# Convolutions that skip time steps by a branch, a written order for TensorE, and a moved set of copies, in a state-space and expert kernel

## The chip, the cores and the metric

The kernel runs on one core of one Trainium2 chip. The core has a matrix engine (TensorE, PE in the profile), a vector engine (VectorE, DVE), a scalar engine (ScalarE, ACT), a general engine (GpSimd, POOL) and an engine that mostly issues transfers (SyncE, SP). They run side by side, each through its own queue in order, and meet at semaphores. Matrix products go to a small memory (PSUM) that the other engines empty. The metric is the device time of one execution in microseconds (us): the median of the runs.

## The reference

The input x has 128 rows of 32 heads with 512 time steps each, and every row has a length. Each head's signal is convolved with a kernel made of 64 decaying waves, the skip term D is added, steps from the row's length on are set to zero, and the 4,096 tokens (row, head) of 512 numbers go through a mixture of 16 experts, of which each token takes 4, and one shared expert. The result is added to x.

```python
K = 2.0 * einsum('hn,hnl->hl', Ct, exp(P)).real          # one kernel per head
y = irfft(rfft(u, 2L) * rfft(K, 2L))[..., :L] + u * D[:, None]
y = y * (arange(L)[None, :] < length[:, None])[:, None, :]
scores = sigmoid(t @ gate_w.T) + bias                    # t: y as 4096 tokens of 512
topk_w, topk_idx = top_k(scores, 4); topk_w = topk_w / sum(topk_w)
out  = sum over the 4 experts e of topk_w[e] * (silu(t @ Wg[e].T) * (t @ Wu[e].T)) @ Wd[e].T
out += silu(t @ Sg.T) * (t @ Su.T) @ Sd.T                # the shared expert
return x + out
```

Lengths are drawn from 78 to 453; the longest of the 128 that are drawn is 443.

## The kernel before

**Kernels of the convolution.** `waves` and `kernels` make the 32 convolution kernels in five chunks (`CHUNKS`): long chains of VectorE operations with some on GpSimd, two sines on ScalarE, small TensorE products (L404), a VectorE addition into `krow` (L412). The result goes to memory (`kd`), and `kernel_strip` reads it back as a strip in which each partition is shifted by one step (L430), four heads at a time. Two strips are kept.

**Convolutions.** The heads go in eight blocks (`tb`) of four (`q`). `load_xt` brings a block of x with time on the partitions (L152). `convolve` multiplies one head: four products (L553) into one PSUM tile `py`, of 512, 384, 256 and 128 columns. The columns are time steps in falling order, column 0 is the last step, so the steps behind a row's end come first. VectorE multiplies the tile by `within`, the zeros behind each row's end (L560). Four transposes by TensorE (L563) with the matrix `to_rank` put the rows in order of length, and ScalarE copies them into `yT` (L564). A finished block goes out to `y_rows` (L899).

**Gates.** Behind a block, `gates` multiplies it by the gate weights (L584, tile `parts`), ScalarE copies that into `by_head`, and `sums` adds it up per head (L601, tile `pg`). Behind every second block `route` picks four experts per token: one long chain of VectorE operations from L623 to L656 (tile `cw`). `weights_out` puts the weights `cw` back into the order of rows by a TensorE product (L664, tile `cw_ps`), which ScalarE copies and SyncE stores in `y_rows` (L669). `ranks` makes small tables from the lengths, among them `k_u` (L512): for each group of 16 rows, how many slices of 128 steps they reach.

**Copies of x.** GpSimd's queue copies x into the output (L903), 1 MB for each block of heads: those of blocks 0 to 3 behind `tb` 3 to 6, the other four behind `tb` 7 (`COPIES`). Everything that is added to the output later waits for them.

**Units and tiles.** Behind the convolutions the shared expert runs in eight units (`unit_step`: `up` L967, `down` L982, added to the output L991), while tables for the sorted tokens are made (`slots`, called `making` there). `up` takes the number of slices from a register that TensorE loads from `k_u` (L1014) and branches on it (`by_tiles`, L942 and L943). Then come the experts: tiles of 128 tokens that share an expert, one `turn_of` each, with a gather four tiles ahead (L932), transposes (L1060, L1110), products (L1092, L1118), and the addition to the output (L1128). 134 tiles are used; those above `NT_MIN` = 128 are run one by one under a condition (`rest`).

**What sets the order.** In the part of the convolutions a scheduler of the tile framework sets each engine's order: it may move an operation past others that don't depend on it, and it does so with TensorE's products. So a `weights_out` that stands right behind `route` in the code is run some heads later. From `unit_step(0)` on the order is written out (`manual_schedule`).

Of the kernel before, what the change touches and what calls it, by code (L numbers as in the profile page):

```python
# [38 lines left out]
P = 128  # L39
# [19 lines left out]
NT_MIN = B * H * TOPK // P  # L59
QC = P // KT  # L60
# [16 lines left out]
def ssm_moe_kernel(  # L77
# [384 lines left out]
    key_col = const.tile([P, 1], F32, tag="key_col", name="key_col")  # L462
    for key, raw, own in ((key_row, key_row, cpos), (key_col, len_col, ppos)):
        nc.vector.tensor_scalar(key, raw, 0.0, float(L), ALU.max, ALU.min)
        if key is key_col:
            num_len = const.tile([P, 2], F16, tag="num_len", name="num_len")
            behind(nc.vector.tensor_copy(num_len[:, 0:1], ppos))
            nc.vector.tensor_copy(num_len[:, 1:2], key)
        nc.vector.scalar_tensor_tensor(key, key, float(P), own, ALU.mult, ALU.subtract)
# [14 lines left out]

    def ranks():
# [7 lines left out]
        nc.vector.tensor_copy(by_rank, by_rank_ps)  # L493

# [15 lines left out]
        nc.tensor.matmul(k_u_ps, lhsT=reach_b, rhs=unit, start=True, stop=True)  # L510
        k_u = const.tile([1, NU], I32, tag="k_u", name="k_u")
# [13 lines left out]
        )  # L525
        row_ps = ps_m.tile([P, NU], F32, tag="m", name="row_ps")
# [14 lines left out]
        return by_rank, reach, k_u, unit_rows  # L541
# [4 lines left out]


    def convolve(tb, q, xt, yb):
        h = tb * HB + q
        py = ps_g.tile([P, L], F32, tag="g", name=f"py{h}")  # L550
        for jt in range(KT):

            nc.tensor.matmul(  # L553
                py[:, : L - jt * P],
                lhsT=xt[:, jt, q, :],
                rhs=strip[tb][:, q, jt * P :],
                start=(jt == 0),
                stop=(jt == KT - 1),
            )
        nc.vector.tensor_mul(yb[:, q, :L], py, within)  # L560
        pt = ps_u.tile([P, KT, P], F32, tag="u", name=f"pt{h}")
        for kt in range(KT):
            nc.tensor.transpose(pt[:, kt, :], yb[:, q, kt * P : (kt + 1) * P], to_rank)  # L563
        return nc.scalar.copy(  # L564
            yT[:, :, :, h, :].rearrange("p u k b -> p k u b"),
            pt.rearrange("p k (u b) -> p k u b", u=NU),
        )
# [307 lines left out]
    xb = load_xt(0)  # L875
    nc.sync.dma_start(out=w_sh, in_=w_all[E])

    COPIES = {3: (0,), 4: (1,), 5: (2,), 6: (3,), 7: (4, 5, 6, 7)}
# [3 lines left out]
    made_waves, strips = {}, [1]  # L882
    for tb in range(NB):
        if tb == 2:
            by_rank, reach, k_u, unit_rows = ranks()
        yb = yp.tile([P, HB, L], F32, tag="yb", name=f"yb{tb}")
        x_next = load_xt(tb + 1) if tb + 1 < NB else None
        for q in range(HB):
            turned = convolve(tb, q, xb, yb)
            h = tb * HB + q  # L890
            if h in waves_at:
                made_waves[waves_at[h]] = waves(*waves_at[h], 0)[0]
            if h in kernels_at:
                kernels(*kernels_at[h], *made_waves[kernels_at[h]])

            if strips[-1] in (tb, tb + 1) and strips[-1] < NB and strips[-1] * HB in kd_of:
                kernel_strip(strips[-1])
                strips.append(strips[-1] + 1)
        nc.scalar.dma_start(out=y_bh[:, tb * HB : (tb + 1) * HB, :L], in_=yb)  # L899

        for part in COPIES.get(tb, ()):
            own = slice(part * HB, (part + 1) * HB)
            x_out = nc.gpsimd.dma_start(out=out_bh[:, own, :], in_=x[:, own, :])  # L903
            dep(x_out, turned, "behind the block")
        gates(tb)
        if tb + 1 < NB:
            sums(tb)
            if tb % RB == RB - 1:
                route(tb // RB)
                weights_out(tb // RB)  # L910
        xb = x_next
# [47 lines left out]
    k_us, adds, loads = {}, [], []  # L959
# [49 lines left out]
    def unit_step(u):  # L1009
# [3 lines left out]
        if u < NU:  # L1013
            k_us[u] = nc.tensor.value_load(k_u[0:1, u : u + 1], min_val=1, max_val=KT)  # L1014
# [135 lines left out]
    with tc.manual_schedule(engines=None):  # L1150
# [37 lines left out]
        for step in range(1, NT_MIN + 2):  # L1188
            turn_of(step)
# [64 lines left out]
```

## Time and profile before

| | us |
|---|---|
| median of 3 runs (933.74 to 934.65) | 934.33 |
| profiled execution | 936.54 |
| its span | 934.8 |
| TensorE busy in the span | 887.1 |
| VectorE busy | 411.9 |
| GpSimd busy | 419.8 |
| start of the first convolution product L553 | 22.66 |
| start of the weights products L664 at blocks 1, 3 and 5 | 69.38, 100.35, 128.32 |
| start of the first product of the units L967 | 138.64 |
| end of the last addition to the output issued by GpSimd | 923.0 |

The span is the time from the first to the last instruction of the profiled execution; what lies around it is the difference to that execution's time, 1.7 us. In rows in order of time the first number is the start in us from the span's start, the second the duration, then come engine, line, operation and tiles; what stands in brackets is how long the engine had stood idle before and what ended that. "x8" says that eight records were merged. A float32 product of TensorE leaves two records. Lines are those of the kernel before.

### The profile page before, as it was taken

To read this page: it belongs to the slowest core of one execution; us is meant where nothing else is said; L and a number is where in the kernel's file an instruction comes from. 1 tells how busy PE (TensorE), PEld (TensorE's weight loads), DVE (VectorE), ACT (ScalarE), POOL (GpSimd) and SP (SyncE) were. 2 spreads that over 40 slices of the span, in tenths; PEclk is the share of its full clock that TensorE was granted. 3 is DMA by queue.
4 is the path that set the end of the run, shared out by engine and by line. 5 is a ranking of instruction groups with operands and counts; after the bars stand their busy time and mean duration, and the time that the engine had idled before them with its cause. 6 is when DMAs were issued, how large, how long until landed. Compare 5 with 4: busy or idle time off the path is not lost.

```text
span 934.8 us, 14577 instructions
## 1 busy us (share of the span) xinstructions
PE 887.1 (95%) x2976; PEld 444.1 (48%) x2976; DVE 411.9 (44%) x1452; ACT 190.2 (20%) x377; POOL 419.8 (45%) x366
## 2 busy tenths in 40 slices
PE   2999979999999999999999999999999999999993
PEld 1555644444444444444444444454445454444441
DVE  8984445677851233423343334333433333344331
ACT  1222221111222122212221122212211112122220
POOL 2200010223456455645564556545655445566553
PEclk9999999999999999999999999999999999999997
DMA  5478955386869666775678567756766656677664
GB/s 202 147 235 270 322 192 163 46 301 127 145 123 238 163 114 116 141 173 106 115 137 184 104 109 137 130 101 110 131 108 114 105 104 112 108 129 137 117 115 85
DMA packets 54689, 135.95 MB, mean 145 GB/s; under 512 B 12416, under 2 KB 12576, under 8 KB 50976
## 3 DMA queue, kind: packets, MB, share of 16 engines
q0 software_dynamic: 36256, 89.77, 52.3%
q1 hardware_dynamic: 14080, 36.15, 11.5%
q10 hardware_dynamic: 4224, 8.39, 2.3%
q8 instruction: 72, 1.18, 0.5%
q14 instruction: 57, 0.47, 0.2%
HBM read 288.08 MB, written 60.64 MB: 373 GB/s over the span
## 4 chain that ended last, share of the span: by engine, by line
PE 67%; issue 1%; SPq 0%; POOL 0%; DVE 0%; ACT 0%; POOLq 0%; DVEq 0%
PE g L1092 34%; PE o L1118 24%; PE m L1060 4%; PE u L1110 3%; PE o L982 1%; POOL out L1128 0%; SPq L1195 0%; POOL yg L932 0%; SPq L1143 0%; DVE zt L1104 0%; SPq L1178 0%; SPq L1179 0%; SPq L1180 0%; ACT sgt L1103 0%; DVE zT L1113 0%
## 5 line engine op out<-in xcount | busy, mean ns | idle before, releaser
L1092 PE MATMUL g<-store,yt 128*128 x742 | 343.1, 596 | 2.0 <-issue 1.7
L1128 POOL DMA_INDIRECT out<-ob,put x134 | 212.1, 1583 | 241.5 <-DVE junk L1067 202.4
L1118 PE MATMUL o<-store,zT 128*128 x536 | 252.0, 592 | 0.1
L1104 DVE SCALAR_TENSOR_TENSOR zt<-g,wt,sgt 128x256 f32<-128x256 f32 x135 | 65.3, 483 | 307.5 <-ACT sgt L1103 307.5
L1092 PEld LDWEIGHTS g<-store,yt 128*128 128x128 f32 x742 | 130.3, 190 | 119.0 <-issue 117.9
L1118 PEld LDWEIGHTS o<-store,zT 128*128 128x128 f32 x536 | 101.5, 190 | 129.0 <-issue 124.6
L932 POOL DMA_INDIRECT yg<-y_rows,get x140 | 138.1, 986 | 42.7 <-issue 29.9
L1127 DVE COPY ob<-o 128x512 f32<-128x512 f32 x134 | 92.7, 692 | 109.5 <-PE o L1118 102.2
L1066 ACT COPY yt<-m 128x512 f32<-128x512 f32 x136 | 79.7, 586 | 225.8 <-PE m L1060 224.0
L1103 ACT ACTIVATE sgt<-g 128x256 f32<-128x256 f32 x135 | 51.9, 384 | 269.7 <-PE g L1092 269.2
L991 POOL DMA_INDIRECT out<-ob,unit_rows x32 | 50.2, 1568 | 99.8 <-ACT ob L989 94.1
L1060 PEld LDWEIGHTS m<-ident,yg 128*128 128x128 f32 x373 | 48.6, 141 | 72.9 <-issue 72.7
L553 PE MATMUL py<-strip,xt 128*128 128x512 f32 (+3 forms) x256 | 76.8, 437 | 2.8 <-DMA strip<-kd 2.8
L1060 PE MATMUL m<-ident,yg 128*128 128x128 f32 x373 | 63.2, 273 | 0.7 <-issue 0.6
L982 PE MATMUL o<-store,z 128*128 128x512 f32 x128 | 57.7, 597 | 1.3 <-ACT yt L1066 1.3
L1113 DVE COPY zT<-u 128x256 f32<-128x256 f32 x134 | 56.3, 420 | 0.4 <-PE u L1110 0.4
L1110 PE MATMUL u<-ident,zt 128*128 128x128 f32 x268 | 51.2, 273 | 0.6 <-DVE zt L1104 0.6
L553 PEld LDWEIGHTS py<-strip,xt 128*128 128x128 f32 x256 | 42.1, 191 | 19.5 <-issue 11.1
L967 PE MATMUL g<-store 128*128 128x512 f32 x92 | 44.8, 623 | 3.1 <-issue 2.6
L967 PE MATMUL u<-store 128*128 128x512 f32 x92 | 42.2, 593 | 0.0
L842 DVE TENSOR_SCALAR cols<-tpos_h,stl,tok 128x143 f16<-128x143 f16 x128 | 41.4, 328 | 0.0
L903 POOL DMA_DIRECT2D out<-in_x x8 | 4.4, 558 | 78.0 <-ACT store L564 78.0
(279 smaller groups left out, 507.5 us busy)
## 6 DMA issues: line engine op xcount, KB each, us to landing
store<-in_w_all SPq DMA_DIRECT2D x143, 1536.0 KB
xt<-in_x_t SPq DMA_DIRECT2D x8, 1024.0 KB
y_rows<-yb ACTq DMA_DIRECT2D x8, 1024.0 KB
out<-in_x POOLq DMA_DIRECT2D x8, 1024.0 KB, 10.1
strip<-kd SPq DMA_DIRECT2D x7, 1024.0 KB
yg<-y_rows,get POOLq DMA_INDIRECT x140, 4.4
out<-ob,put POOLq DMA_INDIRECT x134, 4.9
strip<-kd SPq DMA_DIRECT2D x4, 256.0 KB
```

The costliest lines, as they stand in the source:

```text
L553: nc.tensor.matmul(py[:, : L - jt * P], lhsT=xt[:, jt, q, :], rhs=strip[tb][:, q, jt * P :], start=(jt == 0), stop=(jt == KT - 1),)
L932: nc.gpsimd.indirect_dma_start(out=at(yg, t), out_offset=None, in_=y_rows[:, :], in_offset=bass.IndirectOffsetOnAxis(ap=made["get"][:, t : ...
L967: nc.tensor.matmul(ps[it], lhsT=w_sh[:, c0 : c0 + P], rhs=yT[:, u, kt, :, :].rearrange("p h b -> p (h b)"), start=(kt == KT - n), stop=(kt ...
L982: nc.tensor.matmul(po, lhsT=at(zu, u)[:, it, q * P : (q + 1) * P], rhs=w_sh[:, c0 : c0 + L], start=(it == 0), stop=(it == IT - 1),)
L1060: nc.tensor.transpose(pt[:, q, :], at(yg, t)[:, q * P : (q + 1) * P], ident)
L1066: nc.scalar.copy(at(yt, t), pt)
L1092: mm = nc.tensor.matmul(pgu, lhsT=at(yt, t)[:, q, :], rhs=ring_flat[:, bass.ds(w0s[t] + q * 2 * I, 2 * I)], start=(q == KT - n), stop=(q = ...
L1104: nc.vector.scalar_tensor_tensor(at(zs, t), pgu[:, I:], at(wts, t), sg, ALU.mult, ALU.mult)
L1110: nc.tensor.transpose(at(p_z, t)[:, it, :], at(zs, t)[:, it * P : (it + 1) * P], ident)
L1118: mm = nc.tensor.matmul(po, lhsT=at(zts, t)[:, it, :], rhs=ring_flat[:, bass.ds(w0s[t] + WD + it * L, L)], start=(it == 0), stop=(it == IT ...
L1127: nc.vector.tensor_copy(ob, po)
L1128: add = nc.gpsimd.indirect_dma_start(out=out, out_offset=bass.IndirectOffsetOnAxis(ap=made["put"][:, t : t + 1], axis=0), in_=ob, in_offse ...
```

## The change

Seven things are different.

1. A register `skips` says how many slices of 64 steps (`TS`) lie behind the end of the longest row, 0 to 3. It is worked out from the lengths by a reduction and five small operations of VectorE. From head 2 on `convolve` branches on it (`by_number`, two comparisons) to one of four copies of its products, in which the first 64, 128 or 192 columns are left out. Two fixed PSUM tiles `pys` take the place of a new one for each head, so that columns that are left out hold old finite numbers, which `within` sets to zero.
2. TensorE's order in the part of the convolutions is the written one. Other engines keep the scheduler.
3. The transposes of a head (`turn_y`) stand behind the products of the next head.
4. What follows a head is in `behind_head`: `weights_out` at heads 12, 20 and 28; a step of `ranks` at heads 13 to 16; `gates` of the block before at its second head; `sums` and `route` of the block before at its third head, so `route` comes at heads 10, 18 and 26.
5. The register for `k_u` of unit 0 is loaded before the last head's transposes, no longer in `unit_step`.
6. All eight copies of x are issued behind the last head's transposes.
7. At step 124 GpSimd gets a `drain` ahead of its gather.

```diff
+LAST_DRAIN = NT_MIN - 4
+TS = 64
+SKIPS = 4
@@ the lengths
+        if key is key_row:
+            nc.vector.tensor_reduce(longest, key[0:1, :], AX.X, ALU.max)
...
+    nc.vector.tensor_scalar(longest, longest, -1.0, float(L), ALU.mult, ALU.add)
+    floor_div(longest, longest, TS)
+    nc.vector.tensor_scalar(skips, longest, float(SKIPS - 1), None, ALU.min)
@@ convolve
+    def by_number(m, lo, hi, some):
+        if lo == hi:
+            some(lo)
+            return
+        mid = (lo + hi) // 2
+        with tc.If(m > mid) as more:
+            by_number(m, mid + 1, hi, some)
+        with more.Else():
+            by_number(m, lo, mid, some)
+    pys = [ps_g.tile([P, L], F32, tag="g", name=f"py{i}") for i in range(2)]
...
-        py = ps_g.tile([P, L], F32, tag="g", name=f"py{h}")
-        for jt in range(KT):
-            nc.tensor.matmul(
-                py[:, : L - jt * P],
-                lhsT=xt[:, jt, q, :],
-                rhs=strip[tb][:, q, jt * P :],
...
+        py = pys[h % 2]
+        def products(n):
+            c0 = n * TS
+            for jt in range(KT):
+                nc.tensor.matmul(
+                    py[:, c0 : L - jt * P],
+                    lhsT=xt[:, jt, q, :],
+                    rhs=strip[tb][:, q, jt * P + c0 :],
...
+        if h < 2:
+            products(0)
+        else:
+            if not skip:
+                skip[0] = nc.tensor.value_load(skips[0:1, 0:1], min_val=0, max_val=SKIPS - 1)
+            by_number(skip[0], 0, SKIPS - 1, products)
         nc.vector.tensor_mul(yb[:, q, :L], py, within)
+    def turn_y(h, yb):
+        q = h % HB
         pt = ps_u.tile([P, KT, P], F32, tag="u", name=f"pt{h}")
@@ the loop over the heads
-    COPIES = {3: (0,), 4: (1,), 5: (2,), 6: (3,), 7: (4, 5, 6, 7)}
...
+    def behind_head(h):
+        tb, q = divmod(h, HB)
...
+        if 13 <= h <= 16:
+            next(rest_of_ranks, None)
+        if h >= RB * HB and h % (RB * HB) == HB and h // (RB * HB) > 0:
+            weights_out(h // (RB * HB) - 1)
+        if q == 1 and tb > 0:
+            gates(tb - 1)
+        last = h == H - 1
+        if q == 2 and tb > 0 and not (tb == NB - 1):
+            sums_and_route(tb - 1)
+        if h > 0:
+            turn_y(h - 1, ybs[(h - 1) // HB])
+        if last:
+            sums_and_route(tb - 1)
+            k_us[0] = nc.tensor.value_load(of_ranks["k_u"][0:1, 0:1], min_val=1, max_val=KT)
+            turned = turn_y(h, ybs[tb])
+            gates(tb)
+            return turned
+    def sums_and_route(tb):
+        sums(tb)
+        if tb % RB == RB - 1:
+            route(tb // RB)
+    with tc.manual_schedule(engines={mybir.EngineType.PE}):
+        for h in range(H):
...
+            convolve(tb, q, xbs[tb], ybs[tb])
+            if q == HB - 1:
+                nc.scalar.dma_start(out=y_bh[:, tb * HB : (tb + 1) * HB, :L], in_=ybs[tb])
+            turned = behind_head(h)
+    for part in range(NB):
+        own = slice(part * HB, (part + 1) * HB)
+        x_out = nc.gpsimd.dma_start(out=out_bh[:, own, :], in_=x[:, own, :])
+        dep(x_out, turned, "behind the convolutions")
@@ unit_step
-            k_us[u] = nc.tensor.value_load(k_u[0:1, u : u + 1], min_val=1, max_val=KT)
+            if u > 0:
+                k_us[u] = nc.tensor.value_load(k_u[0:1, u : u + 1], min_val=1, max_val=KT)
@@ the steps
+            if step == LAST_DRAIN:
+                nc.gpsimd.drain(fusable=False)
             turn_of(step)
```

More of the change, by code (lines that the diff above doesn't have):

```diff
@@ L462, in ssm_moe_kernel @@
     key_col = const.tile([P, 1], F32, tag="key_col", name="key_col")
+    longest = const.tile([1, 1], F32, tag="longest", name="longest")
     for key, raw, own in ((key_row, key_row, cpos), (key_col, len_col, ppos)):
         nc.vector.tensor_scalar(key, raw, 0.0, float(L), ALU.max, ALU.min)
+        if key is key_row:
+            nc.vector.tensor_reduce(longest, key[0:1, :], AX.X, ALU.max)
         if key is key_col:
@@ L483, in ssm_moe_kernel @@
     nc.vector.tensor_scalar(to_row, rank_ps[:, :B], ppos, None, ALU.is_equal)
+    of_ranks = {}
     def ranks():
@@ L493, in ranks @@
         nc.vector.tensor_copy(by_rank, by_rank_ps)
+        yield
         reach = const.tile([P, KT], BF16, tag="reach", name="reach")
@@ L510, in ranks @@
         nc.tensor.matmul(k_u_ps, lhsT=reach_b, rhs=unit, start=True, stop=True)
+        yield
         k_u = const.tile([1, NU], I32, tag="k_u", name="k_u")
@@ L525, in ranks @@
         )
+        yield
         row_ps = ps_m.tile([P, NU], F32, tag="m", name="row_ps")
@@ L540, in ranks @@
         )
-        return by_rank, reach, k_u, unit_rows
+        of_ranks.update(by_rank=by_rank, reach=reach, k_u=k_u, unit_rows=unit_rows)
+    skips = const.tile([1, 1], I32, tag="skips", name="skips")
+    nc.vector.tensor_scalar(longest, longest, -1.0, float(L), ALU.mult, ALU.add)
+    floor_div(longest, longest, TS)
+    nc.vector.tensor_scalar(skips, longest, float(SKIPS - 1), None, ALU.min)
     within = const.tile([P, L], F32, tag="within", name="within")
     behind(nc.vector.tensor_scalar(within, lpos, len_col, None, ALU.is_lt))
+    def by_number(m, lo, hi, some):
[8 more added lines that the diff above has]
+    pys = [ps_g.tile([P, L], F32, tag="g", name=f"py{i}") for i in range(2)]
+    skip = {}
     def convolve(tb, q, xt, yb):
         h = tb * HB + q
-        py = ps_g.tile([P, L], F32, tag="g", name=f"py{h}")
-        for jt in range(KT):
-            nc.tensor.matmul(
-                py[:, : L - jt * P],
-                lhsT=xt[:, jt, q, :],
-                rhs=strip[tb][:, q, jt * P :],
-                start=(jt == 0),
-                stop=(jt == KT - 1),
-            )
+        py = pys[h % 2]
[6 more added lines that the diff above has]
+                    rhs=strip[tb][:, q, jt * P + c0 :],
+                    start=(jt == 0),
+                    stop=(jt == KT - 1 or L - (jt + 1) * P <= c0),
+                )
+                if L - (jt + 1) * P <= c0:
+                    break
+        if h < 2:
[4 more added lines that the diff above has]
+            by_number(skip[0], 0, SKIPS - 1, products)
         nc.vector.tensor_mul(yb[:, q, :L], py, within)
+    def turn_y(h, yb):
+        q = h % HB
         pt = ps_u.tile([P, KT, P], F32, tag="u", name=f"pt{h}")
@@ L872, in slots @@
         yield
-    xb = load_xt(0)
-    nc.sync.dma_start(out=w_sh, in_=w_all[E])
-    COPIES = {3: (0,), 4: (1,), 5: (2,), 6: (3,), 7: (4, 5, 6, 7)}
     waves_at = {0: CHUNKS[1], 2: CHUNKS[2], 7: CHUNKS[3], 12: CHUNKS[4]}
     kernels_at = {0: CHUNKS[1], 5: CHUNKS[2], 10: CHUNKS[3], 16: CHUNKS[4]}
[L882 to L911, printed above, removed]
@@ new lines, in ssm_moe_kernel @@
+    made_waves, strips, k_us = {}, [1], {}
+    ybs, xbs, rest_of_ranks = {}, {0: load_xt(0)}, ranks()
+    nc.sync.dma_start(out=w_sh, in_=w_all[E])
+    def behind_head(h):
+        tb, q = divmod(h, HB)
+        if h in waves_at:
+            made_waves[waves_at[h]] = waves(*waves_at[h], 0)[0]
+        if h in kernels_at:
+            kernels(*kernels_at[h], *made_waves[kernels_at[h]])
+        if strips[-1] in (tb, tb + 1) and strips[-1] < NB and strips[-1] * HB in kd_of:
+            kernel_strip(strips[-1])
+            strips.append(strips[-1] + 1)
+        if 13 <= h <= 16:
[15 more added lines that the diff above has]
+            return turned
@@ new lines, in sums_and_route @@
+    def sums_and_route(tb):
[4 more added lines that the diff above has]
+        for h in range(H):
+            tb, q = divmod(h, HB)
+            if q == 0:
+                ybs[tb] = yp.tile([P, HB, L], F32, tag="yb", name=f"yb{tb}")
+                if tb + 1 < NB:
+                    xbs[tb + 1] = load_xt(tb + 1)
+            convolve(tb, q, xbs[tb], ybs[tb])
+            if q == HB - 1:
+                nc.scalar.dma_start(out=y_bh[:, tb * HB : (tb + 1) * HB, :L], in_=ybs[tb])
+            turned = behind_head(h)
@@ L912, in ssm_moe_kernel @@
+    for part in range(NB):
+        own = slice(part * HB, (part + 1) * HB)
+        x_out = nc.gpsimd.dma_start(out=out_bh[:, own, :], in_=x[:, own, :])
+        dep(x_out, turned, "behind the convolutions")
+    by_rank, reach, k_u, unit_rows = (of_ranks[k] for k in ("by_rank", "reach", "k_u", "unit_rows"))
     conv.close()
@@ L958, in ssm_moe_kernel @@
     p_o = homes(ps_o, "o", [P, L], 2)
-    k_us, adds, loads = {}, [], []
+    adds, loads = [], []
     def up(u, it, ps, w0):
```

## The prediction

> **What bounds the kernel now.** I read the stages first: busy time of each engine between the marks of the convolution part (columns: stretch, its length, then PE, weight loads, DVE, ACT and POOL busy with instruction counts, granted clock, DMA share, GB/s).
>
> ```profile
> 17.00:69.40 52.40, 48.36 (x252) 29.42 (x252) 49.05 (x200) 10.79 (x22) 10.30 (x24) 1.00 0.58 188
> 69.40:100.40 31.00, 30.06 (x162) 18.68 (x162) 16.46 (x60) 6.52 (x12) 1.34 (x2) 1.00 0.85 286
> 100.40:128.40 28.00, 26.36 (x131) 16.14 (x131) 14.71 (x50) 6.03 (x11) 1.06 (x2) 1.00 0.82 287
> 128.40:138.70 10.30, 7.08 (x46) 4.02 (x46) 1.38 (x2) 3.10 (x6) 2.04 (x4) 1.00 0.40 117
> 138.70:300.00 161.30, 156.64 (x490) 73.03 (x491) 94.16 (x388) 32.31 (x55) 57.54 (x40) 0.99 0.68 160
> ```
>
> Up to 69.4 us VectorE and TensorE are both nearly full (49.05 and 48.36 of 52.4), after it TensorE alone. From 138.7 on, TensorE is never short of work, and the change touches nothing there but a drain. So a shift of the first product of the units (L967, at 138.64) passes whole to the end, and the question is when that product starts.
>
> Second, the waits of TensorE, which are few: the scheduler has put other work into every gap.
>
> ```profile
> PE pt L563 <- DVE yb L560: 3.2, 4, 1.5
> PE py L553 <- DMA strip<-kd: 2.8, 3, 1.5
> ```
>
> Third, in order of time, TensorE and then VectorE between one `sums` and the `weights_out` that belongs to it:
>
> ```profile
> 113.25 0.96 PE L601 MATMUL pg<-gather_q,by_head 128*128 128x16 f32 x8
> ...
> 121.69 2.97 PE L553 MATMUL py<-strip,xt 128*128 128x384 f32 x10
> 124.50 0.60 PE L563 MATMUL pt<-to_rank,yb 128*128 128x128 f32 x4
> ...
> 128.32 0.49 PE L664 MATMUL cw_ps<-cw,to_row 128*128 128x128 f32 x2
> ```
>
> ```profile
> 114.25 0.29 DVE L623 TENSOR_SCALAR neg<-pg 128x128 f32<-128x128 f32 x1 [0.97 <-PE pg L601]
> ...
> 127.97 0.29 DVE L656 TENSOR_TENSOR cw<-s,free 128x128 f32<-128x128 f32 x1
> ```
>
> `route` is a chain of VectorE operations from L623 to L656. Its parts between the multiplications L560 last 1.92, 2.16, 2.19, 3.15 and 0.73 us, together 10.15. TensorE fills that time with four more heads before it comes to `cw_ps`.
>
> **The change, part by part.** *Shorter products.* The longest of the drawn rows has 443 of 512 steps, so (512 - 443)/64 floors to 1 and heads 2 to 31 leave out 64 columns in each of four products: 1,024 columns for 1,280. From 121.69 to 124.50 TensorE made five products of 1,664 columns: 1.69 ns a column. So a head's products fall from 2.16 to 1.72 us, 0.43 each, 12.9 over 30 heads if TensorE were the bound throughout.
>
> *Start to the first `cw_ps`.* It isn't: VectorE has the same work before that point, plus six one-element operations (about 0.1 each, 0.6), and from 17 us to 69.3 it idles only some 2.4 us in all. In the written order it also waits for TensorE more: the kernel products L404 of the third chunk now stand behind the transposes and products of head 10 (0.44 + 1.72 + 0.5 = 2.7, less 1.5 of VectorE work in between: 1.2), the sums behind those (0.6), and head 7 behind `parts` and sums (0.5). So `cw_ps` starts at 69.38 + 0.6 + 2.3 = 72.3: +2.9, with no gain from shorter products.
>
> *The written order.* `weights_out` is now two heads behind `route` (heads 10 and 12, 18 and 20, 26 and 28). In TensorE's order its product stands ahead of everything later and waits for L656. Between the end of the sums and it TensorE has two heads: 2 x (0.44 + 1.72) = 4.3 us. VectorE needs 10.15 plus three multiplications of 0.6, which stand within its chain: 12.0. TensorE stands still for 7.7 us, queued behind it the transposes of the head before and all products; who waits for those are VectorE's multiplications and ACT's copies. Only at the first of the three does other VectorE work come into it; its wait is about 10 us, already within the 72.3.
>
> From `cw_ps` at head 12 to that at head 20 TensorE does: itself 0.42, six transposes 2.64, six heads 10.32, two `parts` 2.0, two sums 1.62, kernel products 0.62, three small ones 0.3 = 17.9, then the 12.0: 29.9 for 30.97 before (69.38 to 100.35), -1.05. To head 28: 17.0 + 12.0 = 29.0 for 27.97, +1.03. From there to L967: 0.42 + four transposes 1.76 + three heads 5.16 + `parts` 1.0 + sums 0.81 = 9.15; then head 31's transposes to the end of `parts`, 2.37 as before (134.60 to 136.97), and two branches 0.35: 11.9 for 10.32, +1.55. The early load of `k_u` (up to 0.81, below) is in that: it runs under the sums. Both waits for strips fall away, for the copies have left these transfers (three of 1 MB for four in a block); in these sums they aren't counted. Sum so far: 2.9 - 1.05 + 1.03 + 1.55 = +4.4.
>
> *The clock.* What an idle TensorE costs afterwards, the seam of before shows, in stretches of 3.4 us and then in order of time:
>
> ```profile
> 135.60:139.00 3.40, 1.42 (x9) 0.46 (x10) 0.00 (x0) 0.84 (x2) 2.04 (x4) 1.00 0.97 317
> 139.00:142.40 3.40, 3.40 (x5) 1.35 (x4) 0.00 (x0) 0.00 (x0) 0.00 (x0) 0.50 0.95 369
> ```
>
> ```profile
> 138.64 5.39 PE L967 MATMUL g<-store 128*128 128x512 f32 x8 [1.67 <-issue]
> 148.20 3.60 PE L967 MATMUL g<-store 128*128 128x512 f32 x8
> ```
>
> A stretch with 1.42 of 3.4 us busy was followed by one at half clock, and eight records took 5.39 us for 3.60: 1.8 lost. The Trainium skill (TensorE: Matmul & The Clock Gate, "Why this matters for your kernels") asks only that no gap exceed about 3 us; here gaps of 0.68 and 1.67 were enough, so the row decides. By both, each new stop of 7.7 us or more costs about 1.8: 3 x 1.8 = +5.4. By the row alone the seam can also become free: it is now some 70% busy, and a stretch with 2.15 of 3.4 busy (132.2 to 135.6) was followed by full clock: -1.8. By the rule the seam has nothing to win, and the total would be 939.2 where the row gives 937.4. Bounds: 0, and 7.5 if each stop throttles for more than one stretch. Sum: +8.0.
>
> *Branches and loads*, from rows by line (shortest, median, longest ns):
>
> ```profile
> L943 PEldq COMPARE_BRANCH  x364: 65/179/346, 138.5 to 900.3; - x182
> L1198 PEldq COMPARE_BRANCH  x8: 70/73/4495, 892.5 to 925.2; - x8
> L1014 PEldq TENSOR_LOAD <-k_u x8: 302/408/814, 137.2 to 266.3; - x8
> ```
>
> The Trainium skill (Runtime: NRT & Kernel Launch, "Instruction fetch mechanics") warns that a taken branch to code that isn't loaded stops the engine for a fetch. The exit at L1198 shows it, 4.5 us; 30 heads of that would be +135. But L943 jumps over alternatives of this size 364 times at 0.18. I take L943: two branches a head lie under the 2 us of queued products, so nothing; if that cover is gone (behind each stop), 0.3 each, 1 us in all. The load of `skips` comes at head 2, where VectorE is the bound; uncovered it is 0.8.
>
> *Copies of x.* Eight on POOL's queue behind the last transposes, with no POOL work before the units' adds behind them. Before, four took from 137.7 to 151.1 (13.4 us). Eight take some 27 from about 145: 172. The first add, 174.5 before, comes near 182: hidden by 10 us. On SP, each store of weights waits for its `cw_ps`; the loads behind it belong to later blocks and have over 10 us.
>
> *The drain.*
>
> ```profile
> L1239 POOLq DRAIN  x1: 194/194/194, 0.4 to 0.4; - x1
> L1250 POOLq DRAIN  x3: 46/109/5547, 928.1 to 934.2; - x3
> ```
>
> The last 5.55 us of the kernel are a POOL drain, begun when every transfer had landed. The first drain, with none issued, took 0.19. If its time grows with the 314 software transfers since the last drain (140 gathers, 134 + 32 adds, 8 copies), 24 are left behind step 124: 0.6, saving 4.9; if fixed, nothing. I take 4.9, nearer to the first row. The new drain costs POOL about as much at step 124, hidden by four gathers ahead and five `ob` buffers (near 20 us).
>
> Sum: 8.0 - 4.9 = **+3.1 us**. The profiled execution took 936.54 (span 934.8), so 939.6; on the median of 934.33 that is **937.4**.
>
> **Rivals.** *The drain saves nothing*: 942.3. For it: it began with all data landed. *The clock stays up at the stops*, or the stops are shorter by as much: 937.4 - 5.4 = 932.0; for it only that the rule's window and the gaps' place are loose. *The weights don't hold TensorE* (the other side: faster): if the chain after the sums took under 4.3 us, products would bound from head 14 on: 18 x 0.43 = 7.7, strips 2.2, load and clock at the seam 3.0, drain 4.9, less the 0.6: 917. It breaks even with today's 28 us at a chain of 11 us, clock aside; against it stand 10.15 us of VectorE work without one wait. *Copies land late*: if eight take over 38 us, the first adds hold the `ob` buffers and TensorE: 945 or more; the 13.4 us of today's four speak against it.
>
> **How the numbers follow.** Likeliest case 0.45 (937.4, own range 934.5 to 941), fixed drain 0.32 (942.3), clock kept 0.11 (932), no stop 0.06 (917), late copies 0.06 (945). Faster by over 0.2% (under 932.5; 0.2% is about what the three runs can tell): 0.06 and half of 0.11. Within: the other half and the low end of the first, 0.18. The rest is slower. The range leaves out "no stop" and the far end of the late copies: 931.5 to 945.
>
> **What would show it.** TensorE waiting for L656 at its weights product three times, 7 to 10 us each, with half clock behind; no wait for strips; L553's columns at four fifths; L967 near 147; the last drain under 1 us. Wrong if those waits are under 4 us, or VectorE's part before the first of them ends well before 72 us.

## The result and the profile after

The changed kernel takes 948.65 us (median; 947.86 to 949.12). The kernel before takes 934.49 us (median of four). The ratio is 1.0146, with a 95% interval of 1.0126 to 1.0166: 14.2 us slower. The forecast had the sign and most of the mechanism, but its 937.4 us is too low, and the result lies 3.7 us above the upper end of its range.

First, the same stages as before, cut at the same events (the three weights products, now L711, and the first product of the units, now L1036). Columns: stretch, its length, then PE, weight loads, DVE, ACT and POOL busy with instruction counts, granted clock, DMA share, GB/s.

```profile
17.00:76.70 59.70, 45.03 (x238) 29.70 (x238) 48.90 (x206) 9.88 (x21) 10.29 (x24) 0.89 0.62 198
76.70:109.55 32.85, 25.58 (x149) 18.40 (x149) 15.73 (x59) 6.02 (x11) 0.00 (x0) 0.92 0.58 187
109.55:142.00 32.45, 25.17 (x131) 18.03 (x131) 14.75 (x50) 5.96 (x11) 0.00 (x0) 0.87 0.42 141
142.00:155.75 13.75, 12.74 (x71) 8.58 (x71) 2.08 (x3) 3.97 (x8) 1.14 (x2) 0.88 0.21 66
```

Read the lengths against 52.40, 31.00, 28.00 and 10.30 us before, and the clock against 1.00. TensorE's busy time fell by 3.3, 4.5 and 1.2 us in the first three stretches, although part of it was run at half clock. Each of them is nevertheless longer: what was added is idle time of TensorE. In the first stretch VectorE did the same work (48.90 us for 49.05) in 7.3 us more.

The waits of TensorE between 17 and 160 us (what waited, for whom; total us, times, longest) say where the idle time is.

```profile
PE cw_ps L711 <- DVE cw L703: 21.6, 3, 8.7
PE py L587 <- DMA strip<-kd: 3.9, 1, 3.9
PE pt L610 <- DVE yb L604: 1.7, 2, 0.8
```

The first line is the one that the forecast described; these three waits are called the stops below. The second is one that it had ruled out. In order of time, TensorE around head 8 and around the second stop (start, busy, instruction, idle time before it and what ended that):

```profile
46.47 0.61 PE L610 MATMUL pt<-to_rank,yb 128*128 128x128 f32 x4
50.99 3.86 PE L587 MATMUL py<-strip,xt 128*128 128x448 f32 x8 [3.91 <-DMA strip<-kd]
54.64 1.06 PE L610 MATMUL pt<-to_rank,yb 128*128 128x128 f32 x4
55.50 2.51 PE L587 MATMUL py<-strip,xt 128*128 128x448 f32 x8
...
109.55 0.79 PE L711 MATMUL cw_ps<-cw,to_row 128*128 128x128 f32 x2 [6.43 <-DVE cw L703]
110.14 1.06 PE L610 MATMUL pt<-to_rank,yb 128*128 128x128 f32 x4
110.99 3.73 PE L587 MATMUL py<-strip,xt 128*128 128x448 f32 x8
```

A head's eight records take 1.95 us at full clock. Behind both kinds of wait they take up to twice that. The chain on VectorE that the second stop waits for, from its first to its last operation, lasts 12.0 us:

```profile
97.50 0.29 DVE L670 TENSOR_SCALAR neg<-pg 128x128 f32<-128x128 f32 x1 [3.53 <-PE pg L648]
...
109.21 0.29 DVE L703 TENSOR_TENSOR cw<-s,free 128x128 f32<-128x128 f32 x1
```

Last, the drains of POOL (duration in ns: shortest, median, longest; first and last start): the one at step 124, and those at the end.

```profile
L1260 POOLq DRAIN  x1: 8771/8771/8771, 881.1 to 881.1; - x1
```

```profile
L1322 POOLq DRAIN  x3: 109/193/2020, 943.3 to 946.9; - x3
```

Put beside the forecast's sum, by the two profiled executions (us; the forecast's clock term of 1.8 a stop stands where the stop is):

| Part | Forecast | Measured |
|---|---|---|
| start to the first weights product | +2.9 | 69.38 to 76.70: +7.3 |
| to the second | -1.05 + 1.8 | 30.97 to 32.85: +1.9 |
| to the third | +1.03 + 1.8 | 27.97 to 32.44: +4.5 |
| to the first product of the units | +1.55 + 1.8 | 10.32 to 13.76: +3.4 |
| from there to the start of the last add on POOL | -1.8 | 782.78 to 781.68: -1.1 |
| from there to the end | -4.9 | 13.38 to 9.97: -3.4 |
| sum | +3.1 | +12.6 |

The spans differ by the same 12.6 us (934.8 and 947.4).

### The profile page after: what moved, and what is told of

The parts are those of the page before. It is cut to its first block, busy times and chain, and to the rows that moved or that the text cites. A ratio compares the mean times of both kernels' runs of the same rounds, so it can differ in the third digit from the quotient of the medians.

```text
span 947.4 us, 14668 instructions
## 1 busy us (share of the span) xinstructions
PE 881.6 (93%) x2976; PEld 450.0 (48%) x2976; DVE 411.7 (43%) x1458; ACT 189.9 (20%) x377; POOL 419.7 (44%) x366
## 4 chain that ended last, share of the span: by engine, by line
PE 63%; SPq 2%; issue 1%; POOL 0%; DMA 0%; ACT 0%; DVE 0%; POOLq 0%; ACTq 0%
PE g L1162 32%; PE o L1188 23%; PE m L1130 4%; PE u L1180 3%; PE o L1051 1%; SPq L1213 1%; SPq L1248 0%; SPq L1249 0%; SPq L1250 0%; DMA yg<-y_rows,get 0%; POOL out L1198 0%; SPq L1267 0%; SPq L987 0%; POOL yg L1001 0%; ACT yt L1136 0%
## 5 line engine op out<-in xcount | busy, mean ns | idle before, releaser
L1198 POOL DMA_INDIRECT out<-ob,put x134 | 212.1, 1583 | 235.1 <-DVE junk L1137 183.4
L1188 PEld LDWEIGHTS o<-store,zT 128*128 128x128 f32 x536 | 101.6, 190 | 128.7 <-issue 123.8
L587 PE MATMUL py<-strip,xt 128*128 128x192 f32 (+7 forms) x256 | 70.1, 420 | 4.0 <-DMA strip<-kd 3.9
L587 PEld LDWEIGHTS py<-strip,xt 128*128 128x128 f32 x256 | 48.3, 206 | 25.2 <-issue 19.7
L1036 PE MATMUL g<-store 128*128 128x512 f32 x92 | 43.0, 602 | 1.7 <-issue 0.9
L1036 PE MATMUL u<-store 128*128 128x512 f32 x92 | 42.2, 593 | 0.0
```

What stands on the lines that cost most here:

```text
L587: nc.tensor.matmul(py[:, c0 : L - jt * P], lhsT=xt[:, jt, q, :], rhs=strip[tb][:, q, jt * P + c0 :], start=(jt == 0), stop=(jt == KT - 1 o ...
L1036: nc.tensor.matmul(ps[it], lhsT=w_sh[:, c0 : c0 + P], rhs=yT[:, u, kt, :, :].rearrange("p h b -> p (h b)"), start=(kt == KT - n), stop=(kt ...
L1188: mm = nc.tensor.matmul(po, lhsT=at(zts, t)[:, it, :], rhs=ring_flat[:, bass.ds(w0s[t] + WD + it * L, L)], start=(it == 0), stop=(it == IT ...
L1198: add = nc.gpsimd.indirect_dma_start(out=out, out_offset=bass.IndirectOffsetOnAxis(ap=made["put"][:, t : t + 1], axis=0), in_=ob, in_offse ...
```

## The experiments

Each run has executions of the kernel before beside it (their medians are 934.6 to 935.4 us), and its ratio is to those. A difference to the changed kernel, or between two runs, is one of medians that were not taken side by side; by the intervals of the ratios it is sure to some 3 us.

### Where the loss comes from: the stops

The first edit moves only the three weights products in the written order. To 16, 24 and 31, since behind head 31 the order ends:

```
-        if h >= RB * HB and h % (RB * HB) == HB and h // (RB * HB) > 0:
-            weights_out(h // (RB * HB) - 1)
+        if h in (16, 24, 31):
+            weights_out((16, 24, 31).index(h))
```

> The changed kernel with the three weights products in the written order three to four heads later (behind heads 16, 24 and 31 for 12, 20 and 28); all else as changed. Theory (the written order makes the loss): the three waits for VectorE at that product (8.70, 6.43 and 6.44 us, 21.6 in all) go, and with them the half clock behind each (some 1.0 to 1.8 us a head, about 4 in all): 948.6 - 25, about 924. The first wait need not go whole, as VectorE is nearly full before it. Rival (the stops are only where the slack shows; VectorE and the strips' transfers bound the stretch): the waits turn up again at the multiplications or the strips, and the time stays above 938.

It took 922.14 us, 0.9869 of the kernel before (0.9845 to 0.9892): 26.5 us less than the changed kernel, and faster than the kernel before. Its waits of TensorE:

```profile
PE py L587 <- DMA strip<-kd: 4.1, 1, 4.1
...
PE cw_ps L711 <- DVE cw L703: 2.3, 3, 1.1
```

The 21.6 us at the weights products have become 2.3, and the units start at 130.8 instead of 155.75 us. The rival, that the idle time would turn up elsewhere and the time stay above 938 us, is out. The wait for the strip is still there.

The opposite edit drops the written order and leaves the placing to the scheduler, branches included.

```
-    with tc.manual_schedule(engines={mybir.EngineType.PE}):
+    with nullcontext():
         for h in range(H):
```

> The changed kernel without the written order: the scheduler places TensorE's instructions, branches included, as in the kernel before; it puts the first weights product six heads behind the sums instead of two. Shorter products, copies, drain as changed. Theory (the order, not the shorter products, is the loss): no wait above 2 us at the weights products, the time below before's, about 922 to 930. Rival (branches in the way of the scheduler, or the branches themselves, cost what the shorter products win): 935 to 945. Rival (the order isn't the loss): about 948.

It took 937.73 us, 1.0028 of the kernel before (1.0019 to 1.0038). This gives back 10.9 of the 14.2 us and misses the theory's 922 to 930. In its TensorE, around the third weights product:

```profile
122.77 1.02 PE L648 MATMUL pg<-gather_q,by_head 128*128 128x16 f32 x8
...
126.79 1.21 PE L610 MATMUL pt<-to_rank,yb 128*128 128x128 f32 x8 [0.24 <-ACT store L611]
135.47 0.80 PE L711 MATMUL cw_ps<-cw,to_row 128*128 128x128 f32 x2 [7.47 <-DVE cw L703]
```

The scheduler put that product behind the last head and ahead of the last `parts` and sums. All heads were done at 128 us, `cw` came at 135.4, and TensorE stood for 7.47 us. It then ran at a clock of 0.50 until the units (135.4 to 143.0). There is also a strip wait of 3.09 us at 39.77, with half clock behind it. The sums from which this chain starts were placed late as well: they stand at 122.77, with one head's products left behind them, and the chain ran from 123.8 to 135.4. So the scheduler's order too has a place where the chain has too little work beside it; the written one of the changed kernel has three.

### The first stretch: the strip at head 8

The strip of heads 8 to 11 is one transfer of 1 MB. The changed kernel issues it at 44.57 us, the kernel before at 45.35, so it isn't later. But TensorE comes to head 8 at 47.1 us instead of 50.85: its products are shorter, and the kernel products of the third chunk no longer stand ahead. First the kernel before (head 8, then the issues of this strip, of the next block of x and of the next strip), then the issues in the changed one:

```profile
50.85 2.32 PE L553 MATMUL py<-strip,xt 128*128 128x512 f32 x8
45.35 0.37 SPq L430 DMA_DIRECT2D strip<-kd  x1
49.25 0.33 SPq L152 DMA_DIRECT2D xt<-in_x_t  x1
49.63 0.43 SPq L430 DMA_DIRECT2D strip<-kd  x1
```

```profile
44.57 0.37 SPq L433 DMA_DIRECT2D strip<-kd  x1
46.67 0.33 SPq L155 DMA_DIRECT2D xt<-in_x_t  x1
47.05 0.43 SPq L433 DMA_DIRECT2D strip<-kd  x1
```

The edit fetches this one strip head by head:

```
-        each = 1 if tb == 0 else HB
+        each = 1 if tb in (0, 2) else HB
```

> The changed kernel with the strip of the third block (heads 8 to 11) fetched in four transfers of one head each instead of one of four; all else as changed. Theory (the first stretch is 7.3 us longer because TensorE stands 3.9 us before head 8 for this strip, and then runs it and head 9 at half clock, 1.9 + 0.6 us more, and VectorE and the sums come late by as much): the wait falls to about 1 us, the first weights product comes some 4 us earlier, the total is 3 to 5 us less: about 944.5. Rival (VectorE alone sets the first weights product, its work simply takes until 76.7 in this order): the wait falls but the product stays at 76 to 77, 948 to 949. Rival (four small transfers are slower to land than one): no shorter wait, 948 or more.

It took 944.90 us, 1.0108 of the kernel before (1.0081 to 1.0135), 3.75 us less than the changed kernel. The theory said 3 to 5, but the two intervals overlap a little; the trace is clearer than the total. In its TensorE:

```profile
49.00 2.02 PE L587 MATMUL py<-strip,xt 128*128 128x448 f32 x8 [0.81 <-DMA strip<-kd]
...
72.46 0.80 PE L711 MATMUL cw_ps<-cw,to_row 128*128 128x128 f32 x2 [9.23 <-DVE cw L703]
```

The wait fell from 3.91 to 0.81 us, the head behind it runs at full clock, and the first weights product comes at 72.46 us instead of 76.70. That is the 72.3 us which the forecast had worked out without a wait for a strip. Three traces with the single transfer and this order have the product at 75.32, 76.70 and 76.82 us, so such a point is good to about a microsecond, and the 4.2 us are clear of that. VectorE's work is not what took until 76.7.

The single transfer also took longer than before. In the kernel before 1.04 MB moved between 46.25 and 50.00 us. By this estimate the strip's 1.05 MB had landed at about 50.0, 4.7 us behind its issue and 0.8 us before TensorE came. In the changed kernel the first product started 6.4 us behind the issue, and 1.39 MB moved between 45.5 and 51.0. The next x and the next strip are issued when head 7's products end, and that is now only 2.1 us behind this strip's issue instead of 3.9. In the five traces with a single transfer and a wait, head 8 started 6.4 to 6.7 us behind the issue where the next x followed within 1.5 to 2.1 us, and 5.5 us where it followed after 2.6 (the full-length run below). Had the strip taken 4.7 us, about 2.2 of the 3.9 us of waiting would be left. That the rest comes from the company of these transfers is argued from these rows; no run holds them back.

Does the short product win anything ahead of this point? Here all heads are computed at full length, without branches (`products(0)` for every head):

```
-        if h < 2:
+        if True:
             products(0)
```

> The changed kernel with every head's products at full length and no branch: 1,280 columns a head for 1,024; all else as changed. Theory (shorter products count only where TensorE bounds, outside the heads that lie in a stop's cover, and before head 8 they only lengthen the wait for a strip): 18 heads x 0.43 = 7.7 us slower, less some 2 to 3 us of the strip wait and half clock at head 8 that go away: about 953 to 954, and the wait for the strip at head 8 under 2 us instead of 3.9. Rival (products bound throughout): 948.6 + 12.9 = 961. Rival (nothing is won by the short products at all in this order): 948.6 or less.

It took 954.94 us, 1.0194 of the kernel before (1.0156 to 1.0231), 6.3 us more than the changed kernel. The intervals overlap, for one of its four executions took 947.77 us and the others 954.78 to 956.01; the trace is of one of the latter. In its TensorE:

```profile
52.65 4.09 PE L587 MATMUL py<-strip,xt 128*128 128x512 f32 x8 [2.26 <-DMA strip<-kd]
...
76.79 0.79 PE L711 MATMUL cw_ps<-cw,to_row 128*128 128x128 f32 x2 [6.86 <-DVE cw L703]
```

The first weights product is where it was (76.79 for 76.70). The 64 columns left out in the heads before it win nothing there that these traces can show: the wait for the strip and the stop, together 9.1 us here, are 12.6 in the changed kernel. The 6.6 us by which the units start later (162.4 us) arise behind it: 1.8, 2.5 and 2.2 us in the three later stretches. Six, six and three heads lie there outside the stops' cover, and at about 0.36 us a head (below) they make 5.4 of it. The forecast's sums had counted just these. The wait for the strip fell to 2.26 us, where under 2 was expected.

### The clock behind the stops

To keep TensorE busy in a stop without moving anything, products of constants go ahead of the weights product in TensorE's order. Their result is not used. First 20 at each stop:

```
+        if rb < NB // RB - 1:
+            fill = ps_u.tile([P, KT, P], F32, tag="u", name=f"fill{rb}")
+            for n in range(FILL):
+                nc.tensor.matmul(
+                    fill,
+                    lhsT=ones,
+                    rhs=ones.unsqueeze(1).to_broadcast([P, KT, P]),
+                    ...
         cw_ps = ps_m.tile([P, nh * E], F32, tag="m", name=f"cw_ps{rb}")
```

> The changed kernel with 20 products of constants (128x512 bf16, as in the warming loop at the start, 0.29 us each there: 5.9 us) ahead of each of the three weights products in the written order; their result goes nowhere. Theory (the stops halve the granted clock behind them, and that costs time of its own): the stops keep their ends, clock 1.00 behind them, heads behind them 1.95 us for 3.13, 3.73 and 2.92: 4 to 5 us faster, about 944. Rival (the clock behind a stop costs nothing because VectorE is late anyway, or the clock falls for another reason): 948.6 or slower by what the products add.

It took 945.76 us, 1.0107 of the kernel before (1.0086 to 1.0128). The 20 took 4.48 us rather than 5.9, so 4.4, 1.9 and 2.1 us of the stops stayed open. The second of these:

```profile
107.83 0.49 PE L722 MATMUL cw_ps<-cw,to_row 128*128 128x128 f32 x2 [1.90 <-DVE cw L704]
108.15 0.60 PE L611 MATMUL pt<-to_rank,yb 128*128 128x128 f32 x4
108.59 3.15 PE L588 MATMUL py<-strip,xt 128*128 128x448 f32 x8
111.67 1.50 PE L632 MATMUL parts<-store,gw 128*32 128x512 f32 x8
```

The weights product is at full clock (0.49), but the head behind it takes 3.15 us for 1.95: a remaining gap of 1.90 us was still followed by half clock, only later. So the kernel was run with enough of them, 37, 27 and 27 (the edit is against the run with 20):

```
-FILL = 20
+FILL = (37, 27, 27)
-            for n in range(FILL):
+            for n in range(FILL[rb]):
```

> As the run with 20 products of constants at each stop, with enough of them (37, 27 and 27 at 0.224 us, as those 20 took 4.48) to leave less than 0.5 us of each stop open. Theory (half clock behind a stop is its own cost, and 1.9 to 2.1 us left open were still enough for it): clock 1.00 behind all three; against the changed kernel's trace the first head behind them is 1.2, 1.8 and 1.0 us shorter, the weights product and transposes 0.7 each: 6 us less than the changed kernel, about 942.7. Rival (only some of it counts, as in the run with 20): 945 to 946, with the time lost again at VectorE's chains. Rival (the prediction's 1.8 a stop): 943.2, not to be told from the first by the total, but by the heads' times.

It took 943.19 us, 1.0085 of the kernel before (1.0068 to 1.0102), 5.5 us less than the changed kernel. Behind the same stop:

```profile
107.94 0.49 PE L722 MATMUL cw_ps<-cw,to_row 128*128 128x128 f32 x2 [0.17 <-DVE cw L704]
...
108.71 1.95 PE L588 MATMUL py<-strip,xt 128*128 128x448 f32 x8
```

All three heads behind the stops took 1.95 us. Three stops cost 5.5 us through the clock by the medians, and 5.9 by the two traces; the forecast had 5.4. The stops themselves keep their length, since VectorE sets it.

### The other two parts of the change, alone

The drain at step 124 put into the kernel before, and nothing else:

```
+            if step == LAST_DRAIN:
+                nc.gpsimd.drain(fusable=False)
             turn_of(step)
```

> The kernel before with the POOL drain at step 124 and nothing else. Theory (the last drain's time grows with the software transfers since the last one, on top of a part that stays): its drain falls from 5.55 to about 2.0 us as in the changed kernel, 934.3 - 3.5 = 930.8. The prediction's own term: to 0.6 us, 929.4. Rival (fixed, the gain in the changed kernel came from elsewhere, or the new drain holds POOL and the adds): 934.3 or above.

It took 932.23 us, 0.9969 of the kernel before (0.9960 to 0.9978): 2.9 us less. The last drain takes 2.02 us, as in the changed kernel, and the one at step 124 takes 8.00 us at 865 us. Its cover held only in part. POOL stood for 6.97 us before the next gather. The add ahead of the drain started 1.57 us earlier than before (the profiled execution of before had lost 1.7 us to half clock at the start of the units), the last add only 0.88 us. The other traces say the same. From the units' first product, run at full clock, to the last add it is 780.7 us without such a drain (the run with the copies alone, below), 780.4 with one at step 64, and 780.8 to 781.7 in the eight kernels with one at step 124. So this drain gives back about 0.7 us of what it saves at the end.

How the last drain depends on the transfers since the one before it was the open size. The same at step 64:

> The kernel before with the drain at step 64 instead of 124: about 144 software transfers left behind it, for 24 at step 124 and 314 without one. Theory (the last drain has a part that stays and one that grows with those transfers; a line through the two that are known, 2.02 us at 24 and 5.55 at 314): 3.48 us for the last drain. Rival (any earlier drain leaves the same short one): 2.02. Rival (only the first few transfers count, or it is full again after some number): 5.55.

The last drain of this kernel took 4.55 us (one execution of 933.92 us beside 934.63 for the kernel before). 144 software transfers stood behind the earlier drain, 24 with step 124.

```profile
L1253 POOLq DRAIN  x3: 109/194/4552, 926.3 to 931.8; - x3
```

And at step 128, in the fastest kernel so far (below):

> Later weights products and strip by heads (916.1) with the earlier drain at step 128 instead of 124, some 12 to 16 software transfers left behind it for 24. Theory (each transfer up to 144 adds to the last drain: (4.55 - 2.02)/120 = 0.021 us; the earlier one of some 8 us is still hidden by the gathers ahead): last drain 1.7 to 1.85 us, the time unchanged within 0.3 us, 916. Rival (a short drain costs 2.02 in any case): 2.02. Rival (so near the end the earlier drain's 8 us aren't hidden any more: the adds behind it come late): 918 to 923.

There 16 transfers were left:

```profile
L1322 POOLq DRAIN  x3: 46/258/1367, 910.9 to 913.3; - x3
```

By the traces, the drain takes 0.19 us with no transfer before it, 1.37 with 16, 2.02 with 24 (in all ten kernels with the drain at step 124), 4.55 with 144 and 5.55 with 314 (in two). It grows with the transfers, steeply at first and slowly later. The time since the drain before grows with them, so that the count is the cause, and not this time, is not shown. The forecast's straight line from 0 to 314 gave 0.6 us at 24. The theory for 16 here, another straight line, gave 1.7 to 1.85 and is off too, as was that for 144 (3.48).

The eight copies of x behind the convolutions in the kernel before, and nothing else:

```
-        for part in COPIES.get(tb, ()):
-            ...
+    for part in range(NB):
+        own = slice(part * HB, (part + 1) * HB)
+        x_out = nc.gpsimd.dma_start(out=out_bh[:, own, :], in_=x[:, own, :])
+        dep(x_out, turned, "behind the convolutions")
```

> The kernel before with all eight copies of x behind the last head and nothing else. Theory (copies are hidden in either place, but for the waits for strips): the three waits for strips of before (2.8 us in all) go, the first add still finds its copy done, 934.3 - 1 to -3: about 932.5. Rival (the waits for strips come from the strips' own late issue): 934.3, no difference. Rival (eight copies in one go land after the first add could start and hold the results back): 936 or more.

It took 933.09 us, 0.9983 of the kernel before (0.9975 to 0.9991): 1.7 us less. The waits for strips (2.8 us in all) are gone, and the units start at 136.8 for 138.64 us. In the changed kernel the eight copies took from 154.6 to 183.5 us, 28.9 us, and the first add started at 189.9. They are hidden, by 6.4 us.

### What the change can be worth

Later weights products and the strip by heads together:

> Later weights products and the strip by heads together. Theory: with the stops gone TensorE is the bound behind head 8, so the wait there (4.1 us) and the half clock behind it (1.7 us) go straight to the end: 922.1 - 4 to -6, about 917. Rival (VectorE then bounds, and the wait shows up at the multiplications): 921 to 922.

It took 916.06 us, 0.9796 of the kernel before (0.9776 to 0.9815). The stages between the same events:

```profile
17.00:74.10 57.10, 53.93 (x320) 36.47 (x320) 50.46 (x217) 12.96 (x26) 10.24 (x24) 1.00 0.67 216
74.10:97.50 23.40, 22.56 (x134) 16.27 (x132) 14.22 (x52) 5.96 (x11) 0.00 (x0) 1.00 0.84 263
97.50:118.10 20.60, 19.53 (x112) 13.65 (x111) 13.74 (x50) 5.37 (x10) 0.00 (x0) 1.00 0.58 202
118.10:123.20 5.10, 4.05 (x27) 2.14 (x27) 0.60 (x1) 1.71 (x4) 1.90 (x4) 0.80 0.69 219
```

TensorE is busy nearly throughout, at full clock in the first three stretches, and the units start at 123.2 us. The edit of the strip is worth 6.1 us here, and this time the intervals lie apart; whether that is more than its 3.75 with the stops present, these runs can't tell. With the drain at step 128 the same kernel took 914.28 us, 0.9778 of the kernel before (0.9761 to 0.9794), the fastest of all. The two intervals overlap, so the 1.8 us between the medians is not resolved; the drain accounts for 0.65 of it. Its seam, the passage from the convolutions to the units, happened to run at full clock; that of the kernel with step 124 did not (4.38 us for the first eight records of L1036, for 3.69).

What do the shorter products bring there? The edit of the full-length run, in this kernel:

> Later weights products and strip by heads (916.1), with every head's products at full length and no branch. Theory (without stops TensorE is the bound from about head 8 on, so each head behind it is worth its 0.36 to 0.43 us, those before it, where VectorE is nearly full, less): 24 x 0.4 = 9.6 slower, up to 12.9: 925.5 to 928.5. Rival (VectorE or the chain of sums and route bounds also there, shorter products are worth as little as in the changed kernel): under 921.

It took 922.18 us, 0.9860 of the kernel before (0.9844 to 0.9877). So they are worth 6.1 us where TensorE bounds, between the rival's limit and the theory's 9.6. Two stretches from its middle:

```profile
74.00:97.00 23.00, 23.00 (x130) 15.01 (x130) 12.63 (x43) 5.54 (x11) 0.00 (x0) 1.00 0.73 230
97.00:118.00 21.00, 21.00 (x111) 14.63 (x110) 10.77 (x32) 4.86 (x9) 0.00 (x0) 1.00 0.73 247
```

With full heads TensorE has no idle time at all there. With short ones 0.84 and 1.07 us stay idle, in waits for VectorE's multiplications and for the weights. A head with its transposes comes every 2.60 us full and every 2.23 to 2.26 short, 0.36 apart rather than 0.43. Whether the 0.07 us are the branches or the smallest products was not separated.

## Why the prediction was right and wrong

**The stops, right in kind.** TensorE waited three times at the weights product for L703 (the old L656), 8.70, 6.43 and 6.44 us, where 10, 7.7 and 7.7 were worked out. The chain from the end of the sums took 12.0 us in the second and third case, the forecast's 10.15 plus three multiplications. The stops are shorter than forecast because the two heads beside the chain take more than the 4.3 us put for them: 0.84 us of waiting for a multiplication, which lies within the chain, is among it. Moving the products takes the loss away, which is the proof.

**"Both waits for strips fall away": the step that failed.** The forecast put the waits for strips at nothing, and argued from the transfers alone: copies leave, strips come sooner. The waits of the kernel before did go that way (the run with the copies alone). But the first copy of the kernel before is issued at 80.3 us, long after the strip of head 8, so that strip had nothing to gain. And the forecast never asked when TensorE would now reach head 8: 3.8 us sooner, where the strip had landed only some 0.8 us ahead of it. TensorE waited 3.9 us, ran heads 8 and 9 at half clock for 2.5 us more (3.86 and 2.51 for 1.95 each), and VectorE, the sums and the first weights product were late by it. The term was +2.9, measured +7.3. With the wait nearly gone it was 72.46 - 69.38 = +3.1. That this meets the forecast's 2.9 so well may be luck, as its three parts (1.2, 0.6 and 0.5) were not measured one by one, and its 2.4 us of VectorE's idle time are 3.3 by the row that it shows. The strip alone would have made 941.8 of 937.4, still within the range; it took the smaller misses below to leave it.

**The periods.** These are the times from one weights product to the next, and from the third to the units. The forecast's periods without the clock were 29.9, 29.0 and 11.9 us. With the stops filled they are 31.1, 30.0 and 12.1 (76.82, 107.94, 137.92, 150.02). So 2.4 us were missing, most of it in TensorE's own part. In the first of these periods TensorE takes 18.9 us up to the end of the second sums, where 17.9 were put: the six heads take 11.05 for 10.32 from start to start (1.79 to 1.88 us each, not 1.72), the two sums 1.86 for 1.62. Behind it come 12.2 for 12.0. With the clock the periods are 32.9, 32.4 and 13.8, another 5.9 us by the traces.

**The clock, right.** A stop costs 1.8 us: 5.5 for three by the timed runs. The forecast's row was right once more, where the Trainium skill (TensorE: Matmul & The Clock Gate, "Why this matters for your kernels") asks only for gaps of no more than about 3 us: half clock came behind a gap of 1.90 us. The seam's -1.8 is less sure. It ran at full clock in the changed kernel's profile (3.69 us for eight records), but so it did in the kernel before with the drain alone, whose TensorE order there is the same:

```profile
139.11 3.69 PE L968 MATMUL g<-store 128*128 128x512 f32 x8 [1.83 <-issue]
```

In the profiled execution of before the same eight took 5.39 us behind a gap of 1.67. So half clock there is a matter of the execution, and the credit need not be in the medians. The profiled execution of before was 2.2 us above its median, that of the changed kernel (949.08) 0.4 above: that accounts for the 1.6 us between +12.6 and +14.2. The clock goes with it. Of 69 executions of the kernel before that were run beside the experiments, 18 have a mean granted clock of 0.995 and a median of 934.0 us, and 11 one of 0.992, as the profiled execution has, and a median of 936.5. That it is the seam that lost the clock in those 11 is argued from the profiled one, not shown.

**Branches, right.** Ninety branches (L570; three for each of 30 heads, where the forecast had two) took 70 to 435 ns and the load of `skips` 0.49 us. The short products win more than the branches cost: without the stops, where the intervals lie apart, full heads without any branch take 6.1 us more.

```profile
L570 PEldq COMPARE_BRANCH  x90: 70/176/435, 29.1 to 148.5; - x90
```

Of the +135 us that 30 stalls like the 4.5 us at L1198 would have been, nothing occurred. The Trainium skill (Runtime: NRT & Kernel Launch, "Instruction fetch mechanics") speaks of a taken branch whose target isn't loaded, and none of the 90 shows such a stall.

**The drain, right in kind, wrong in size.** It grows with the transfers, but is 2.02 us at 24 rather than 0.6. The -4.9 was -3.4 in the traces, -2.9 in the timed run of the drain alone; the 0.7 us that the drain at step 124 gives back, which the forecast had put at nothing, lie about there. The rival of a fixed drain falls.

**The copies, right.** They took 28.9 us for 27, hidden by 6.4 for 10. The forecast's 13.4 us for the four of before run from the issue of the last of them (137.7); the first was issued at 136.15, so 15 us stood there for four.

By size the miss of 9.5 us in the profiled sum is: 4.4 the strip and what follows from it, 2.4 the periods, 0.5 the clock, 0.7 between the units' start and the last add (about what the drain at step 124 costs there), 1.5 the drain at the end. Between 937.4 and 948.65 lie 11.3; what is left of them is nearly all the profiled execution of before, treated above.

## What to carry to other kernels

When work on one engine gets shorter, ask of every input of that engine not whether it now comes sooner, but whether it comes before the engine's new, earlier time: a transfer that nobody waited for in the old trace may have had next to no slack (0.8 us here, by estimate), and a wait for it also costs the clock behind it. The faster engine also releases later transfers sooner, and they move beside the one that is needed first. In an order written by hand, a product that waits for a chain on another engine belongs behind as many blocks as cover the whole chain: here three to four heads later turned +1.5% into -1.3%. If a last drain is long, an earlier one that is mostly covered pays, and its place counts at both ends.

## What the runs showed of the hardware that was not expected

- Half clock came behind gaps of 1.90 and 2.12 us with products before and behind, and not always behind 1.67 to 1.83: the same seam ran at half clock in one execution and at full clock in others. Behind a gap of 0.68 us the seam ran at half clock in the fastest kernel with the drain at step 124, and at full clock with it at step 128, in the same order of TensorE. So the gap before a product does not decide it alone.
- A POOL drain took 0.19 us at the start, with no transfer before it, and at the end 1.37, 2.02, 4.55 and 5.55 us with 16, 24, 144 and 314 software transfers since the last drain. One in mid-stream took 7.6 to 9.0 us, and at step 124 delayed the last add by about 0.7.
- Four transfers of 256 KB in place of one of 1 MB let the first head start some 3 us sooner after the issue: 49.00 - 45.60 = 3.4 us from the first issue (3.3 in two other traces), for 50.99 - 44.57 = 6.4 us with the single one.
